# A graph network's own terms kept in on-chip memory, and its input tests moved one layer later

## The chip, the cores and the metric

The kernel runs on one core of a Trainium2 chip. The metric is the device time of one execution in microseconds; the median of nine runs before the change is 1521.09 us (1512.48 to 1530.87). TensorE (PE) multiplies matrices; VectorE (DVE), ScalarE (ACT) and GpSimd (POOL) do elementwise work; SyncE (SP) only issues transfers, and ACT and POOL issue some too, each on a queue of its own.

## The reference

Three graph layers run over 6250 nodes with 128 features and 200000 edges sorted by their target `dst`. Layer 0 is a message-passing layer with edge features, layers 1 and 2 are mean-aggregating (SAGE) layers inside a residual block:

```python
h = relu(layernorm(x))
x = x + relu(concat([h, segsum(h[src], dst), segsum(edge_attr, dst)]) @ W.T + b)
h = relu(layernorm(x))
h = relu(segsum(h[src], dst) / max(deg, 1) @ W1_l + b1 + h @ W1_r)      # layer 1
x = x + relu(segsum(h[src], dst) / max(deg, 1) @ W2_l + b2 + h @ W2_r)  # layer 2
```

Everything is float32. `dst` is drawn as 6250 times the square of a uniform number, so low nodes have many edges and high nodes few.

## The kernel before

**Blocks.** The nodes are cut into 49 blocks of 128. In a first phase (the build, up to about 600 us) the kernel counts on the chip how many edges lead from each node to each node, writes these counts to DRAM (`counts_d`), three counts packed in one 32-bit word, and sums the edges' features per target node into `aggE`, a tile of 128 partitions (features) by 49 x 128 nodes and some more columns. `aggE` lies in on-chip memory for the whole kernel.

**The three layers.** A layer's aggregation for a target block is a sum over the 49 source blocks of a matmul of counts with features. Forty blocks (`dense_order`) are done so in `neighbours` (L899): 49 matmuls (L944) of 256 columns, since each feature is split into a high and a low part (`terms`). The counts of a block come in one load of 1088 KB (`fetch`, L836, on SyncE's queue, four blocks ahead) and are cast from bytes to floats (`wide`, L876) by DVE and ACT in six pieces. The nine highest blocks have few edges; their rows are gathered by GpSimd (`gather`, L1025, 447 gathers in all) and summed by short matmuls (`sum_rows`, L1067) that are put among the dense ones at steps written out by hand (`at_step`, L1105). A gather waits for one of four buffers to be free.

**A block's chain.** `after` (L961) is a generator whose parts are issued at fixed steps of the next block. DVE adds the two halves of the sum (`y`, L969), multiplies by one over the degree and adds the *own part* `r` (L984; in layer 0 a plain add, L972). In layer 1 ACT applies Relu (`h`, L993), TensorE transposes `h` (L460), ACT copies it (`hT`, L462), and `times_weights` (L465) multiplies it by the two weight matrices of the next layer side by side (L467). The left half becomes that layer's features (`feats`, written to `rows_d` for the gathers), the right half plus the bias is the own part of that layer for the same block. In layer 2 nothing follows but Relu, the old `x` added, and the transfer to `out` on ACT's queue (L1004). So layer 2 has no transposes and no products behind its sums.

**The own part before.** Layer n makes the own part of layer n+1 in a buffer of three (`r`, L469), writes it to `r_d` in DRAM on SyncE's queue (L474), and `fetch_own` (L848) reads it back (`own`, L853) two blocks before layer n+1 adds it, also on SyncE's queue. There are 49 of these writes and 49 of these reads for each of the three layers, 64 KB each.

**aggE's uses.** In layer 0 one matmul per block multiplies the block's columns of `aggE` by the edge weights (L941, L1081). After layer 0 its first 4704 columns serve as scratch memory for the tests.

**The tests.** The build assumes things about the sorted edge list (how far targets spread within a stretch of edges, that the list is sorted, and more). `windows_right` (L1131) tests these: it loads the list of targets twice (784 KB each) into `aggE`, loads short rows into a small tile, and takes differences and maxima on DVE. It is a generator of 23 steps; one step is issued per dense block of layer 1, from the third on, behind that block's sum. Its transfers and three memsets are on GpSimd's queue, and `later` (L1010) puts each behind the newest gather. `all_right` (L1228) joins all tests to one bit, which goes to DRAM and back; it is issued early in layer 2, in three steps. At the 33rd dense block of layer 2 the engines load the bit (`trip`), and if it is set a slow general version computes everything again. With the inputs timed here it is not set.

**The order.** Every engine works through its instructions in the order in which they are written. A transfer that waits holds up all that stands behind it in its queue. Extra dependencies without a wait (`IN_ORDER`, `issue_after`) keep an instruction behind another of its engine.

Of the kernel before, what the change touches and what calls it, by code (L numbers as in the profile page):

```python
# [9 lines left out]
F32 = mybir.dt.float32  # L10
# [3 lines left out]
I32 = mybir.dt.int32  # L14
# [31 lines left out]
TESTS = 0  # L46
# [41 lines left out]
def kernel(ctx: ExitStack, tc: tile.TileContext, x, srcl, dstl, edge, w0t, b0, w1l, b1, w1r, w2l, b2, w2r, out):  # L88
# [11 lines left out]
    nc = tc.nc  # L100
# [6 lines left out]
    GU = G * U  # L107
    NR = len(REGIONS)
# [44 lines left out]
    r_d = [dram.tile([NP, D], F32, name=f"r{i}_d") for i in range(3)]  # L153
# [17 lines left out]
    unit_d = dram.tile([GU + 2], F32, name="unit_d")  # L171
    at_d = dram.tile([GU], F32, name="at_d")
# [9 lines left out]
    work = fast.enter_context(tc.tile_pool(name="work", bufs=2))  # L182
# [44 lines left out]
    at = once.tile([1, G, U], F32, name="at")  # L227
# [31 lines left out]
    for key, t in [*pick.items(), *pick_l.items()]:  # L259
        n = key if isinstance(key, int) else key[0]  # L260
        e = 16 * n
# [8 lines left out]
        empty = -(-unused // (P * n))  # L270
# [35 lines left out]
    apart = lambda t: t.rearrange("p (u g) -> p u g", u=U)  # L306
# [125 lines left out]
    def moments(xt):  # L432
        st = small.tile([P, 6], F32, name="st")
        nc.vector.bn_stats(st, xt)
        mv = small.tile([P, 2], F32, name="mv")
        nc.vector.bn_aggr(mv, st)
        return mv
# [27 lines left out]
    def times_weights(layer, b, hT, pz):  # L465
        at = slice(b * P, (b + 1) * P)
        mm = nc.tensor.matmul(pz, hT, w_sb[layer], start=True, stop=True)  # L467
        nc.scalar.copy(feats[:, slot_of[b], :], pz[:, :D])
        r = work.tile([P, D], F32, name="r", bufs=3)  # L469
        nc.vector.tensor_tensor(r, pz[:, D:], b_sb[layer], op=ALU.add)  # L470

        def write():
            nc.scalar.dma_start(rows_d[layer][at, :], feats[:, slot_of[b], :])
            nc.sync.dma_start(r_d[layer][at, :], r)  # L474

        return mm, write

# [221 lines left out]
    before = None  # L699
# [5 lines left out]
    for si, (g0, ng, n, w, k, sw, win) in enumerate(stretches):  # L705
# [6 lines left out]
        for g in range(g0, g0 + ng):  # L712
# [37 lines left out]
            for j in range(0, len(live), 2):  # L750
# [28 lines left out]
                for i, t0 in enumerate(units):  # L779
# [8 lines left out]
                    add = nc.gpsimd.tensor_tensor(to, to, fore[:, i, :], op=ALU.add)  # L788
# [25 lines left out]
        before = ring  # L814
# [19 lines left out]
    loaded, wide, own, sums, chains, waiting = {}, {}, {}, {}, {}, []  # L834
# [13 lines left out]
    def fetch_own(i):  # L848
        if isinstance(i, int) and i >= len(blocks):
            return  # L850
        layer, b = block_of(i)
        r = work.tile([P, D], F32, name="own", bufs=4)
        nc.sync.dma_start(r, r_d[layer][b * P : (b + 1) * P, :])  # L853
        own[i] = r

    def block_of(i):
        return blocks[i] if isinstance(i, int) else i
# [103 lines left out]
    def after(i):  # L961

        layer, b = block_of(i)
        at = i % NC if isinstance(i, int) else -1
        ps, r = sums.pop(i), own.pop(i)
        if layer == 0:
            nc.vector.tensor_copy(deg[:, b : b + 1], ps[:, NK * D : NK * D + 1])
        y = work.tile([P, D], F32, name="y", bufs=3)
        nc.vector.tensor_reduce(y, ps[:, : NK * D].rearrange("p (k f) -> p f k", k=NK), AX.X, ALU.add)  # L969
        if layer == 0:  # L970
            xt = xts.pop(i)
            nc.vector.tensor_tensor(y, y, r, op=ALU.add)  # L972
            nc.vector.scalar_tensor_tensor(xt, y, 0.0, xt, op0=ALU.max, op1=ALU.add)
            nc.sync.dma_start(x1_d[b * P : (b + 1) * P, :], xt)
            mv = moments(xt)
            yield
            pair = deviations(mv)
            yield
            next_layer(1, b, normed_to_rows(xt, pair), at < 0)
            if at == NC - 1:  # L980
                nc.vector.tensor_scalar(rdeg, deg, 1.0, None, op0=ALU.max)
                nc.vector.reciprocal(rdeg, rdeg)
            yield
        add = nc.vector.scalar_tensor_tensor(y, y, rdeg[:, b : b + 1], r, op0=ALU.mult, op1=ALU.add)  # L984
        if layer == 1:
            if at == TESTS:
                tests.append(windows_right())
            with tc.issue_after(add.ins):
                if at > TESTS + 1:
                    next(tests[0], None)  # L990
            yield
            h = work.tile([P, D], F32, name="h")
            nc.scalar.activation(h, y, AF.Relu)  # L993
            next_layer(2, b, h, at < 0)
            yield
            yield
        if at == 0:
            tests.append(all_right())
        elif at > 2:
            next(tests[1], None)  # L1000
        xt = xts.pop(i)
        nc.vector.scalar_tensor_tensor(xt, y, 0.0, xt, op0=ALU.max, op1=ALU.add)
        n = P if b + 1 < NB else last
        nc.scalar.dma_start(out[b * P : b * P + n, :], xt[:n, :])  # L1004
        yield
# [2 lines left out]
        (tail_waiting if listed else waiting).append((layer, b, h))  # L1008

    def later(it):  # L1010
        tc.add_manual_dep(it.ins, latest["POOL"].ins.name, IN_ORDER, reason="the first layer goes before the tests")
        return it


    latest, events, alone, tail_waiting, gathered, ready, tail_sums, tail_chain = {}, {}, {}, [], {}, {}, {}, []
# [93 lines left out]
    for layer in range(3):  # L1109
# [5 lines left out]
        for m, (_, _, marks) in enumerate(batches):  # L1115
            s = begin + (end - begin) * m // (len(batches) - 1)
# [14 lines left out]
    def windows_right():  # L1131

        dst, far = aggE[:, :GU], aggE[:, GU : 2 * GU]
        later(nc.gpsimd.dma_start(dst.bitcast(I32), dstl))
        yield
        nexts = aggE[:, 2 * GU : 3 * GU].bitcast(I32)
        later(nc.gpsimd.memset(nexts[P - 32 :, GU - U :], PAD))
        yield
        later(nc.gpsimd.dma_start(nexts[: P - 1, :], dstl[1:, :]))
        yield  # L1140
        later(nc.gpsimd.dma_start(nexts[P - 1 :, : GU - U], dstl[0:1, U:]))
        yield
        if unused:
            first_of_last = bass.AP(
                tensor=dstl.tensor, offset=dstl.offset + pad_p * GU + (G - 1) * U, ap=[[0, 1], [1, 1]]
            )
            later(nc.gpsimd.dma_start(nexts[P - 1 :, GU - 2 * U : GU - 2 * U + 1], first_of_last))
            yield


# [1 line left out]
        RU = RUN * U  # L1152
        assert NR * RU == GU
        rows = late.tile([NR, 5, RU], F32, name="rows")
        for i in range(3):
            later(nc.gpsimd.dma_start(rows[:, i], unit_d[i : i + GU].rearrange("(r e) -> r e", e=RU)))
            yield
        later(nc.gpsimd.dma_start(rows[:, 3], at_d.rearrange("(r e) -> r e", e=RU)))
        yield
        apart = 4  # L1160
        first_rows = (NR - 1) * RU
        later(nc.gpsimd.dma_start(
            rows[: NR - 1, 4], unit_d[1 + apart : 1 + apart + first_rows].rearrange("(r e) -> r e", e=RU)
        ))
        yield
        later(nc.gpsimd.dma_start(
            rows[NR - 1 :, 4, : RU - U - apart], unit_d[1 + apart + first_rows : 1 + GU - U].rearrange("(r e) -> r e", r=1)
        ))
        nothing = late.tile([1, U], F32, name="nothing")
        later(nc.gpsimd.memset(nothing, 0.0))  # L1170
        yield
        beyond = late.tile([1, U + apart], F32, name="beyond")
        later(nc.gpsimd.memset(beyond, float(2 * NP)))
        later(nc.gpsimd.dma_start(rows[NR - 1 :, 4, RU - U - apart :], beyond))
        yield
        nc.vector.tensor_copy(dst, dst.bitcast(I32))
        if unused:
# [41 lines left out]
        if unused:  # L1219

            empty = unused // P
            nc.gpsimd.dma_start(rows[NR - 1 :, 0, RU - U + 1 : RU - U + 1 + empty], nothing[:, :empty])
        yield
        yield
        for i, k in enumerate((0, 1, 3, 4)):
# [2 lines left out]
    def all_right():  # L1228

        highest = small.tile([P, 2], F32, name="highest")  # L1230
        nc.vector.tensor_reduce(highest[:, 0:1], worse, AX.X, ALU.max)
        nc.vector.tensor_reduce(highest[:, 1:2], deg, AX.X, ALU.add)
        yield
        for k, op in ((0, ALU.max), (1, ALU.add)):
            pf = psum.tile([P, 512], F32, name="pf", tag="pz")
            nc.tensor.transpose(pf[:1, :P], highest[:, k : k + 1], ident)
            nc.vector.tensor_reduce(bad[:, 4 + k : 5 + k], pf[:1, :P], AX.X, op)
        nc.vector.tensor_scalar(bad[:, 5:6], bad[:, 5:6], float(E), None, op0=ALU.not_equal)
        nc.vector.tensor_scalar(bad, bad, 0.5, None, op0=ALU.is_gt)
        again = small.tile([1, 1], F32, name="again")  # L1240
        nc.vector.tensor_reduce(again, bad, AX.X, ALU.max)
        again_i = small.tile([1, 1], I32, name="again_i")
        nc.vector.tensor_copy(again_i, again)
        yield
        again_d = dram.tile([1, 1], I32, name="again_d")
        nc.sync.dma_start(again_d, again_i)
        nc.sync.dma_start(trip_i, again_d)
# [18 lines left out]
    tests = []  # L1266
# [266 lines left out]
```

## Time and profile before

| | |
|---|---|
| median of nine runs | 1521.09 us |
| the profiled execution | 1519.39 us, span 1517.8 us |
| build | up to about 600 us |
| adds of the own part in layer 0 (L972), first to last | 605.1 to 906.3 us |
| first add of layer 1 (L984) | 920.1 us |
| layer 2, first to last out transfer | 1230.4 to 1513.0 us |
| tests in layer 1 | 937.7 to 1111 us |
| transfers on SyncE's queue: counts, own parts written, own parts read | 119 of 1088 KB, 147 of 64 KB, 147 of 64 KB |

The span runs from the first to the last recorded instruction. A view over a stretch of time gives, per engine, the busy time and in brackets the number of instructions; for TensorE that number divided by the length is the rate at which it really moves, because the length of one matmul in the records overlaps with the next. In lists of waits a line reads: who waited, at which line of the kernel, for whom, the total in us, how often, the longest. "issue" means that the profile shows nothing that the engine waited for.

### The profile page before, as it was taken

How to read it: one execution, taken by the hardware profiler on the slowest of the kernel's cores; microseconds unless marked ns; L12 is line 12 of the kernel's file. 1: busy time of each engine (PE TensorE's matmuls, PEld its weight loads, DVE VectorE, ACT ScalarE, POOL GpSimd, SP SyncE). 2: the span in 40 equal slices, each digit the busy share in tenths (PEclk: the TensorE clock that was granted, in tenths of full speed). 3: DMA queues.
4: the chain of work that ended last, by engine and by line, in shares of the span. 5: the costliest groups of instructions: out<-in, count | busy, mean ns of one | idle time of the engine just before them, and what ended most of it. 6: DMA issues, size and time to landing. Idle time of an engine off the chain costs nothing.

```text
span 1517.8 us, 37444 instructions
## 1 busy us (share of the span) xinstructions
PE 1426.7 (94%) x12457; PEld 1385.2 (91%) x12457; DVE 1151.1 (76%) x3006; ACT 931.6 (61%) x2253; POOL 685.5 (45%) x921
## 2 busy tenths in 40 slices
PE   7999999899999998999999997999899999998997
PEld 6899999798999997999899996999899989998897
DVE  8888899788998998677677774668666767675664
ACT  5434445467777777676676775666666766564563
POOL 4445667200000001666565605676666246576570
PEclk9999999999999999999999999999999999999999
DMA  2889898788999998777777765766666666676672
GB/s 79 283 267 300 279 322 319 270 299 309 311 315 343 332 354 306 264 239 230 233 227 224 234 207 195 241 223 201 205 224 215 199 202 219 215 248 198 213 250 63
DMA packets 173764, 374.02 MB, mean 246 GB/s; under 512 B 29451, under 2 KB 118985, under 8 KB 154234
## 3 DMA queue, kind: packets, MB, share of 16 engines
q1 hardware_dynamic: 121454, 268.72, 52.7%
q0 software_dynamic: 22336, 88.52, 17.2%
q10 hardware_dynamic: 29772, 14.31, 3.3%
q8 instruction: 100, 1.64, 0.4%
q14 instruction: 102, 0.84, 0.2%
HBM read 289.32 MB, written 82.13 MB: 245 GB/s over the span
## 4 chain that ended last, share of the span: by engine, by line
PE 66%; DMA 17%; issue 8%; DVE 3%; ACT 3%; another core or an unknown queue 1%; ACTq 0%; DVEq 0%; POOLq 0%; SPq 0%; POOL 0%
PE ps L944 43%; DMA counts_d<-ring 16%; PE pe L642 10%; PE ps_t L1077 4%; PE pz L467 3%; PE pu L755 2%; ACT wide L876 1%; PE pt L366 1%; PE pu L467 1%; PE pz L460 1%; DVE wide L876 1%; DMA src_i<-in_src 0%; DMA edge_t<-in_edge 0%; PE ps L941 0%
## 5 line engine op out<-in xcount | busy, mean ns | idle before, releaser
L944 PE MATMUL ps<-terms,wide 128*128 128x256 f32 (+1 forms) x5760 | 814.7, 293 | 19.8 <-issue 16.1
L944 PEld LDWEIGHTS ps<-terms,wide 128*128 128x128 f32 x5760 | 755.7, 200 | 30.0 <-issue 21.9
L1031 POOL DMA_INDIRECT rows_t<-rows_d,row_i x447 | 497.9, 1114 | 375.5 <-issue 112.6
L642 PE MATMUL pe<-hot,edge_t 128*128 128x128 f32 x3136 | 473.6, 288 | 3.1 <-DMA edge_t<-in_edge 2.0
L642 PEld LDWEIGHTS pe<-hot,edge_t 128*128 128x128 f32 x3136 | 396.3, 193 | 6.4 <-issue 2.2
L876 ACT CAST wide<-c 128x1024 fp32r<-128x1024 uint8 x239 | 284.7, 1205 | 131.5 <-PE ps L944 92.7
L781 ACT CAST ring<-pu 128x170 f32 (+5 forms) x736 | 205.7, 282 | 91.2 <-PE pu L766 44.9
L876 DVE CAST wide<-c 128x1024 fp32r<-128x1024 uint8 x241 | 174.2, 725 | 113.3 <-PE ps L944 89.8
L755 PE MATMUL pu<-sq,sp 128*128 128x102 bf16 (+7 forms) x1416 | 171.1, 219 | 15.5 <-DVE r L470 5.2
L876 ACT CAST wide<-c_early 128x1024 fp32r<-128x1024 uint8 x118 | 140.6, 1210 | 72.3 <-PE ps L944 54.1
L808 POOL DMA_DIRECT2D counts_d<-ring x50 | 27.3, 545 | 297.0 <-ACT ring L781 210.8
L788 POOL TENSOR_TENSOR ring<-ring,fore 128x17 int32 x280 | 118.4, 423 | 84.3 <-ACT fore L776 40.2
L520 DVE TENSOR_TENSOR sq<-iota,q_e 128x816 bf16<-128x816 f16 (+7 forms) x177 | 123.6, 699 | 8.5 <-PE pu L766 8.0
L876 DVE CAST wide<-c_early 128x1024 fp32r<-128x1024 uint8 x122 | 88.0, 722 | 55.4 <-PE ps L944 41.4
L755 PEld LDWEIGHTS <-sp 128*128 128x128 bf16 x1416 | 119.5, 99 | 10.4 <-DVE sq L531 3.5
L520 DVE TENSOR_TENSOR sp<-iota,p_e 128x1024 bf16<-128x1024 f16 x177 | 121.9, 688 | 4.5 <-PE pu L755 2.1
L1055 DVE TENSOR_TENSOR tw<-rows_t,tw 128x384 fp32r<-128x384 f32 x153 | 83.1, 543 | 33.6 <-ACT tw L1048 31.0
L766 PE MATMUL pu<-sc,sp 128*128 128x17 bf16 x745 | 96.2, 173 | 0.0
L633 DVE TENSOR_TENSOR hot<-iota,rel 128x64 f32<-128x64 f16 (+13 forms) x196 | 94.7, 485 | 0.0
L1077 PE MATMUL ps_t<-tw,hot_t 128*128 128x256 f32 (+1 forms) x483 | 85.5, 286 | 2.8 <-issue 2.8
L1049 DVE TENSOR_TENSOR hot_t<-iota_p,slot_e 128x384 fp32r<-128x384 f16 (+1 forms) x153 | 87.3, 571 | 0.0
L790 ACT CAST ring<-pu 128x68 f32 (+5 forms) x280 | 63.3, 248 | 38.1 <-ACT fore L776 15.3
(198 smaller groups left out, 1406.6 us busy)
## 6 DMA issues: line engine op xcount, KB each, us to landing
edge_t<-in_edge SPq DMA_DIRECT2D x196, 512.0 KB
c<-counts_d SPq DMA_DIRECT2D x80, 1088.0 KB
c_early<-counts_d SPq DMA_DIRECT2D x39, 1088.0 KB
rows_d<-feats ACTq DMA_DIRECT2D x147, 64.0 KB
r_d<-r SPq DMA_DIRECT2D x147, 64.0 KB
own<-r_d SPq DMA_DIRECT2D x147, 64.0 KB
counts_d<-ring POOLq DMA_DIRECT2D x5, 1462.0 KB
rows_t<-rows_d,row_i POOLq DMA_INDIRECT x447
```

Of the source, the lines that this page charges most:

```text
L520: made = nc.vector.tensor_tensor(to.rearrange("p t (c two) -> p t c two", two=2), iota[:, :m].rearrange("p (c two) -> p c two", two=2).uns ...
L633: nc.vector.tensor_tensor(hot[:, : U * win].rearrange("p (u w) -> p u w", w=win), iota[:, :win].unsqueeze(1).to_broadcast([P, U, win]), re ...
L642: mm = nc.tensor.matmul(ps[:, :P], e[:, u, :], hot[:, u * win : u * win + P], start=u == 0, stop=u == U - 1)
L755: mm = nc.tensor.matmul(pu[:, i * HALF : i * HALF + nq], sp[:, t, :], sq[:, t, :nq], start=t == t0, stop=t == t0 + n - 1 and n > 1,)
L766: mm = nc.tensor.matmul(pu[:, i * HALF : i * HALF + NJ], sp_b[:, t, :], sc[:, slot + 1 - len(last_tiles) + j0, :NJ], start=False, stop=j0 ...
L781: put = nc.scalar.copy(ring[:, bass.ds(to_put[(g - g0) * U + t0], nq)], pu[:, i * HALF : i * HALF + nq])
L788: add = nc.gpsimd.tensor_tensor(to, to, fore[:, i, :], op=ALU.add)
L876: copied = copy(t[:, : p1 - p0], two)
L944: dense = nc.tensor.matmul(ps[:, :m], counts, terms_of(s, s + 1)[:, 0, :m], start=s == 0, stop=s == NB - 1)
L1031: it = nc.gpsimd.indirect_dma_start(out=rows[:, u, :], out_offset=None, in_=rows_d[layer][:, :], in_offset=bass.IndirectOffsetOnAxis(ap=ro ...
L1049: made = nc.vector.tensor_tensor(hot[:, :k, :], iota_p.unsqueeze(1).to_broadcast([P, k, P]), slot_e[:, e : e + k].unsqueeze(2).to_broadcas ...
L1077: mm = nc.tensor.matmul(ps[:, :width], hot[:, k, :], tw[:, u, :width], start=begins, stop=ends)
```

## The change

The own part of layer 1 is written into the block's columns of `aggE` instead of a buffer, and read from there; its 49 writes to DRAM and 49 reads are not issued. Layers 0 and 2 keep theirs. As `aggE` now holds own parts until layer 1 is over, the tests of the edge list move to layer 2: one step per dense block from the third on, behind its sum; when `windows_right` has ended, the steps of `all_right` follow, also one per block. All transfers of the tests go on SyncE's queue instead of GpSimd's, without the order behind the gathers; the three memsets stay on GpSimd behind the newest gather.

```diff
         nc.scalar.copy(feats[:, slot_of[b], :], pz[:, :D])
-        r = work.tile([P, D], F32, name="r", bufs=3)
+        r = aggE[:, at] if layer == 1 else work.tile([P, D], F32, name="r", bufs=3)
         nc.vector.tensor_tensor(r, pz[:, D:], b_sb[layer], op=ALU.add)

         def write():
             nc.scalar.dma_start(rows_d[layer][at, :], feats[:, slot_of[b], :])
-            nc.sync.dma_start(r_d[layer][at, :], r)
+            if layer != 1:
+                nc.sync.dma_start(r_d[layer][at, :], r)
...
         layer, b = block_of(i)
+        if layer == 1:
+            own[i] = aggE[:, b * P : (b + 1) * P]
+            return
         r = work.tile([P, D], F32, name="own", bufs=4)
         nc.sync.dma_start(r, r_d[layer][b * P : (b + 1) * P, :])
...
         add = nc.vector.scalar_tensor_tensor(y, y, rdeg[:, b : b + 1], r, op0=ALU.mult, op1=ALU.add)
         if layer == 1:
-            if at == TESTS:
-                tests.append(windows_right())
-            with tc.issue_after(add.ins):
-                if at > TESTS + 1:
-                    next(tests[0], None)
             yield
             h = work.tile([P, D], F32, name="h")
             nc.scalar.activation(h, y, AF.Relu)
             next_layer(2, b, h, at < 0)
             yield
             yield
-        if at == 0:
-            tests.append(all_right())
-        elif at > 2:
-            next(tests[1], None)
+        if at == TESTS:
+            tests.extend((windows_right(), all_right()))
+        with tc.issue_after(add.ins):
+            if at > TESTS + 1:
+                if next(tests[0], True):
+                    next(tests[1], None)
         xt = xts.pop(i)
...
-        later(nc.gpsimd.dma_start(dst.bitcast(I32), dstl))
+        (nc.sync.dma_start(dst.bitcast(I32), dstl))
         yield
         nexts = aggE[:, 2 * GU : 3 * GU].bitcast(I32)
         later(nc.gpsimd.memset(nexts[P - 32 :, GU - U :], PAD))
         yield
-        later(nc.gpsimd.dma_start(nexts[: P - 1, :], dstl[1:, :]))
-        yield
-        later(nc.gpsimd.dma_start(nexts[P - 1 :, : GU - U], dstl[0:1, U:]))
+        (nc.sync.dma_start(nexts[: P - 1, :], dstl[1:, :]))
+        yield
+        (nc.sync.dma_start(nexts[P - 1 :, : GU - U], dstl[0:1, U:]))
         yield
...
         later(nc.gpsimd.memset(beyond, float(2 * NP)))
-        later(nc.gpsimd.dma_start(rows[NR - 1 :, 4, RU - U - apart :], beyond))
+        (nc.sync.dma_start(rows[NR - 1 :, 4, RU - U - apart :], beyond))
         yield
```

The other seven transfers of `windows_right` change their queue in the same way; its DVE operations are unchanged.

More of the change, by code (lines that the diff above doesn't have):

```diff
@@ L1010, in later @@
     def later(it):
-        tc.add_manual_dep(it.ins, latest["POOL"].ins.name, IN_ORDER, reason="the first layer goes before the tests")
+        tc.add_manual_dep(it.ins, latest["POOL"].ins.name, IN_ORDER, reason="the third layer's gathers go before the tests")
         return it
@@ L1146, in windows_right @@
             )
-            later(nc.gpsimd.dma_start(nexts[P - 1 :, GU - 2 * U : GU - 2 * U + 1], first_of_last))
+            (nc.sync.dma_start(nexts[P - 1 :, GU - 2 * U : GU - 2 * U + 1], first_of_last))
             yield
@@ L1155, in windows_right @@
         for i in range(3):
-            later(nc.gpsimd.dma_start(rows[:, i], unit_d[i : i + GU].rearrange("(r e) -> r e", e=RU)))
+            (nc.sync.dma_start(rows[:, i], unit_d[i : i + GU].rearrange("(r e) -> r e", e=RU)))
             yield
-        later(nc.gpsimd.dma_start(rows[:, 3], at_d.rearrange("(r e) -> r e", e=RU)))
+        (nc.sync.dma_start(rows[:, 3], at_d.rearrange("(r e) -> r e", e=RU)))
         yield
@@ L1161, in windows_right @@
         first_rows = (NR - 1) * RU
-        later(nc.gpsimd.dma_start(
+        (nc.sync.dma_start(
             rows[: NR - 1, 4], unit_d[1 + apart : 1 + apart + first_rows].rearrange("(r e) -> r e", e=RU)
@@ L1165, in windows_right @@
         yield
-        later(nc.gpsimd.dma_start(
+        (nc.sync.dma_start(
             rows[NR - 1 :, 4, : RU - U - apart], unit_d[1 + apart + first_rows : 1 + GU - U].rearrange("(r e) -> r e", r=1)
@@ L1221, in windows_right @@
             empty = unused // P
-            nc.gpsimd.dma_start(rows[NR - 1 :, 0, RU - U + 1 : RU - U + 1 + empty], nothing[:, :empty])
+            nc.sync.dma_start(rows[NR - 1 :, 0, RU - U + 1 : RU - U + 1 + empty], nothing[:, :empty])
         yield
```

## The prediction

> **What bounds the kernel now.** I read the page first: the span, the busy shares and the chain that ended last.
>
> ```profile
> span 1517.8 us, 37444 instructions
> PE 1426.7 (94%) x12457; PEld 1385.2 (91%) x12457; DVE 1151.1 (76%) x3006; ACT 931.6 (61%) x2253; POOL 685.5 (45%) x921
> ...
> PE 66%; DMA 17%; issue 8%; DVE 3%; ACT 3%; another core or an unknown queue 1%; ACTq 0%; DVEq 0%; POOLq 0%; SPq 0%; POOL 0%
> ```
>
> TensorE sets the pace; SyncE's and GpSimd's queues have 0% of the chain, and its DMA share belongs mainly to the counts that are written during the build (the chain's line for counts_d<-ring, 16%), which the change doesn't touch. So what the edit takes from queues pays only where TensorE waits in the same stage. The second view is therefore the busy time of each engine in stretches of layers 1 and 2, chosen by what the removed and moved steps do in them: 938 to 1110 us holds all the tests of edge lists (the first of their transfers is issued at 937.7, the last reduction runs at 1110.9).
>
> ```profile
> 938.00:950.00 12.00, 4.85 (x20) 3.83 (x19) 4.34 (x9) 3.29 (x6) 6.25 (x8) 0.68 0.42 122
> 950.00:1110.00 160.00, 151.59 (x1182) 148.77 (x1182) 112.97 (x270) 101.65 (x167) 107.72 (x102) 0.98 0.68 219
> 1110.00:1185.00 75.00, 72.19 (x572) 70.75 (x571) 50.03 (x111) 49.96 (x82) 46.13 (x43) 1.00 0.66 218
> 1185.00:1220.00 35.00, 35.00 (x280) 34.51 (x279) 26.18 (x53) 26.29 (x44) 0.93 (x1) 1.00 0.61 202
> ...
> 1220.00:1242.00 22.00, 22.00 (x182) 21.95 (x182) 15.91 (x32) 15.80 (x18) 8.11 (x8) 1.00 0.61 205
> 1242.00:1254.00 12.00, 8.39 (x36) 6.47 (x36) 2.51 (x6) 3.18 (x4) 7.27 (x8) 0.67 0.47 151
> 1254.00:1414.00 160.00, 152.07 (x1192) 150.01 (x1191) 106.06 (x240) 90.07 (x97) 106.77 (x93) 0.96 0.68 225
> ```
>
> The columns after the length are PE, weight loads, DVE, ACT and POOL, each with its count, then the clock, the DMA share and GB/s. Read the counts of PE as a rate. Layer 1 with tests and gathers runs 1182 / 160 = 7.39 matmuls per us, with gathers but no tests 572 / 75 = 7.63, with neither 280 / 35 = 8.00. Both layers open with a stall while the first gathers are issued without a pause: 20 matmuls in 12 us in layer 1, 36 in layer 2. Layer 2 reaches 8.27 per us before that and 7.45 in the 160 us behind it. The third view says what TensorE waits for: in 950 to 1110 us first, then in 1254 to 1414 us.
>
> ```profile
> PE pz L460 <- ACT h L993: 4.6, 2, 2.4
> PE pz L467 <- ACT hT L462: 3.6, 3, 2.1
> ...
> PE ps L944 <- issue: 6.3, 13, 0.9
> PE ps_t L1077 <- issue: 1.5, 2, 0.8
> ```
>
> In layer 1 it waits for a block's own chain (DVE's sum, ACT's Relu and copy, a transpose). Layer 2 has no such chain behind it, and its waits have no releaser at all. That is the asymmetry the forecast turns on.
>
> **The change, part by part.** All times are against the profiled execution: 1517.8 us of span in 1519.4 us, which is 1.7 us under the median of 1521.1.
>
> *49 writes of the own part in layer 0 and 49 reads in layer 1 go.*
>
> ```profile
> L474 SPq DMA_DIRECT2D r_d<-r x147: 235/326/1859, 49.5 to 1226.9; - x147
> L853 SPq DMA_DIRECT2D own<-r_d x147: 319/320/567, 64.7 to 1494.0; - x147
> ```
>
> SyncE loses 98 x 0.32 = 31 us of issuing and the waits for r and y in front of them, and 98 x 64 KB = 6.4 MB of 374 MB leave the transfers, about 26 us at the mean 246 GB/s. All of it lies beside other work: SPq is 0% of the chain, and TensorE's waits name no transfer of the own part. What is behind them on the queue is the load of counts, which takes its place when DVE frees a buffer, so it would only wait there instead. I take 0; the far end is a gain of 2 us, because the chain has one wait of 1.8 us on own<-r_d (at 870 us). The sum of r is the same DVE instruction (0.29 us) into another address; its buffer is the block that the matmul of layer 0 with the edges' weights read about two blocks earlier, so no new wait is late.
>
> *The tests leave layer 1.* On GpSimd that is 12 transfers, 0.57 to 1.16 us each, 7.7 us, and 11 us with the 0.3 us ahead of each; three memsets of 0.1 us move with them. On DVE I add the rows: the cast 0.98, three small ones 0.54, two subtractions 3.57, four maxima of rows 3.7, memsets and small maxima about 1, then 0.51, 1.58 and 1.77, eight operations on 14 rows 2.0 and four maxima 1.0: 16.6 us.
>
> ```profile
> L1189 DVE TENSOR_TENSOR aggE<-aggE,first x2: 1785/1786/1786, 1037.0 to 1052.6; 128x1568 f32<-128x1568 f32 x2
> ```
>
> What they cost TensorE comes from the rates: 1182 matmuls at 7.63 would take 155.0 us, so 5.0 us of 160. The two TensorE waits shown, 8.2 us in this stretch against 1.9 in the 75 us after it, say the same. The opening stall of layer 1 is 12 - 20 / 7.63 = 9.4 us long, that of layer 2, which has no test in it, 12 - 36 / 8.27 = 7.6 us; I give the difference, 1.7 us, to the 784 KB transfer issued at 937.7 among the gathers. Gain taken: 6.7 us. Ends: 0, if both were chance, and 14.4 us if the whole opening stall were that transfer's.
>
> *They arrive in layer 2.* 16.6 us of DVE, three memsets on GpSimd behind its newest gathers, and 12 transfers (1.6 MB) on SyncE at 0.32 us, 4 us of issue, one step per dense block, from the third block. Layer 2 lasts 282 us by its outputs (1230.4 to 1513.0), 7.07 us per dense block, so the 23 steps end near 1408 and the verdict is in memory by about 1425, some 30 us before the 33rd block, where the engines read it. Queued behind a test on SyncE are the own part, the old x and the counts. The two large loads landed 4.3 and 6.6 us after their issue, by the semaphores in the trace; the small one that follows a memset can hold SyncE for about 3 us, what GpSimd was behind DVE in layer 1 (memset at 1022.5, its block's sum at 1020). Cover: a load of counts in layer 2 is issued some 12 us before its first cast (the one issued at 1256.4 is cast from about 1268) and takes 4.6 us (the chain's piece at 688.5), so 7 us are free, and TensorE asks for that cast a block later still. DVE in 1254 to 1414 us is at 106 / 160 = 66%, under the 71% of layer 1's tests; its steps delay ACT's out transfer, and so ACT's casts, by up to 2.9 us in some blocks, under the same cover. Ends: 0, and 6.7 us, the price in layer 1. I take 2, nearer to the free end, because no wait of TensorE in layer 2 names ACT or DVE.
>
> At this place a rule speaks against the change. The Trainium skill, "DMA: Bandwidth & Descriptors", section "Issuing engines are not separate DMA queues", says that transfers issued from different engines end on the same 16 DMA engines and that changing the issuer saves issuing time only. If the cost of the tests is in their transfers, it then moves to layer 2 whole and the sum would be 0 instead of minus 4.7. No view here separates the two; the rates above price the tests as a whole.
>
> *The two steps of the verdict* (two transposes, six small DVE operations, two transfers) move from the start of layer 2 behind the tests: the same instructions in the same layer, 0, covered by the 30 us above.
>
> Sum: 0 - 6.7 + 2 + 0 = -4.7 us: 1514.7 us against the profiled run, **1516.4 us** against the median.
>
> **The rivals.** *The cost only changes its layer (hidden anyway).* Layer 2 charges what layer 1 saves: 0, 1521. For it: layer 2 at 7.45 matmuls per us is already no better than layer 1 without tests. Against it: the waits shown are of different kinds.
>
> *Layer 2's unexplained stalls multiply (slower).* Its rate of 8.27 would need 144 us for the 1192 matmuls that took 160, so 16 us are lost in stalls with no releaser, while GpSimd issues gathers and counts are loaded; the clock column falls to 0.96. If the 1.6 MB and DVE's long operations add half as much again, that is +8; with nothing saved in layer 1, 1529. It decides when the added stalls pass 6.7 us. Against it: layer 0 runs 2284 matmuls in the 300 us from 605 (7.61 per us) at a DMA share of 0.72, higher than layer 2's, with the clock at 1.00.
>
> *The opening stall was the 784 KB load.* All 14.4 us come back and layer 2 charges 2: 1509. Against it: layer 2's opening is nearly as bad without a test.
>
> *The change doesn't do what it says*: if the scheduler took the shared memory for one object, writing r would wait for the last matmul that read any of it; that matmul runs blocks ahead, so it costs nothing here.
>
> **How the numbers follow.** Of 1521, half a per cent is 7.6 us, about what a measurement of this kernel can tell from no change. Forecast, a gain of 2 to 10 us: 0.40. Cost changes its layer, -2 to +5: 0.18. Stalls multiply, +5 to +14: 0.25. Opening stall goes, -10 to -16: 0.17. Of the forecast's share a third (0.13) lies beyond a gain of 7.6, of the stalls' share 0.03 within a loss of 7.6. So faster 0.17 + 0.13 = 0.30, slower 0.22, same 0.48. The forecast's own range is 1511 to 1519. For 8 in 10 the range takes in the fast case to 1506 and the slow one to 1531.
>
> **What would show it.** Right: layer 1 between its opening and the end of its gathers at 7.6 matmuls per us, waits for hT and h near 2 us per 75; own<-r_d and r_d<-r at x98; aggE<-in_dst on SPq in layer 2; layer 2's 160 us behind its opening at 7.35 or more. Wrong: layer 1 still at 7.4, or the issue waits of L944 in layer 2 well above 14 us, or a wait of TensorE for a cast of counts there.

## The result, and the profile after

The changed kernel takes 1542.47 us (median of 20 executions, 1532.97 to 1553.33), the kernel before 1522.98 (62 executions). The ratio is 1.0148 with an interval of 1.0127 to 1.0169 (the two medians alone give 1.0128): slower, by 19 to 26 us on 1522.98. Ratios, here and below, leave out executions more than 1.5% above the fastest of the same kernel. The prediction was 1516.4 us with a range of 1506 to 1531, so its sign and its range are both wrong.

The profiled execution took 1536.36 us, with a span of 1534.8. Its page, the same lines as before:

```profile
span 1534.8 us, 37165 instructions
PE 1430.7 (93%) x12457; PEld 1388.1 (90%) x12457; DVE 1151.2 (75%) x3006; ACT 932.0 (61%) x2253; POOL 692.2 (45%) x909
...
PE 77%; DMA 7%; issue 4%; ACT 4%; DVE 3%; POOL 1%; another core or an unknown queue 1%; ACTq 0%; SPq 0%; DVEq 0%; POOLq 0%
PE ps L948 41%; PE pe L643 21%; PE pu L756 4%; PE ps_t L1078 3%; PE pz L467 3%; DMA counts_d<-ring 3%; DMA c<-counts_d 2%; PE pu L467 2%; ACT ring L782 1%; ACT wide L880 1%; PE pt L366 1%; DMA x_c<-in_x 1%; PE pz L460 1%; DVE wide L880 1%
```

TensorE is busy 4 us longer, the span is 17.0 us longer. New among the chain's large lines is a transfer: `c<-counts_d`, the load of a block of counts, with 2% of the span. The share of the build's `counts_d<-ring` in this chain (16% before, 3% now) says nothing on the change: a chain is one path out of several. (The changed file has a few more lines: L944 of before is L948 here, L876 is L880, L655 is L656, L853 is L857, L1139 is L1140.)

The busy time in stretches shows where the time went. The columns are the stretch, its length, then PE, weight loads, DVE, ACT and POOL with their counts, the clock, the DMA share and GB/s. First layer 1, in the same stretches as before:

```profile
950.00:1110.00 160.00, 152.22 (x1186) 148.57 (x1186) 102.55 (x221) 102.38 (x168) 98.66 (x90) 0.99 0.60 199
1110.00:1185.00 75.00, 74.63 (x592) 73.36 (x592) 50.51 (x110) 52.44 (x88) 45.74 (x42) 1.00 0.67 227
```

With no operation of the tests on DVE or GpSimd in it, the first stretch has 1186 matmuls in 160 us, 7.41 per us, where it had 1182. The expected 7.63 did not come. Then the opening of layer 2:

```profile
1216.00:1241.00 25.00, 24.94 (x206) 24.81 (x205) 16.77 (x34) 16.39 (x19) 11.22 (x11) 1.00 0.69 232
1241.00:1253.00 12.00, 6.36 (x27) 4.79 (x26) 2.71 (x7) 2.56 (x4) 7.69 (x9) 0.70 0.25 68
1253.00:1272.00 19.00, 19.00 (x148) 19.00 (x148) 9.90 (x21) 8.40 (x9) 9.28 (x9) 0.92 0.36 116
1272.00:1294.00 22.00, 0.86 (x6) 0.66 (x5) 2.75 (x6) 3.56 (x4) 0.16 (x1) 0.60 0.36 123
1294.00:1414.00 120.00, 118.27 (x945) 116.07 (x945) 97.50 (x242) 72.59 (x79) 93.19 (x73) 0.99 0.72 241
```

The stall of 1241 to 1253 was there before. The one of 1272 to 1294 is new: TensorE does 6 matmuls in 22 us, and behind it runs at 945 / 120 = 7.88 per us, though DVE does the tests there. The waits from 1254 to 1300 us (engine and line, what it waited for, us in total, times, longest) name the cause:

```profile
ACT wide L880 <- DMA c<-counts_d: 24.6, 1, 24.6
DVE wide L880 <- DMA c<-counts_d: 24.0, 1, 24.0
...
PE ps_t L1078 <- DVE tw L1056: 21.1, 1, 21.1
```

One wait, once: ACT and DVE wait for a load of counts. Each works in order. The gathered rows' high parts (`tw`, L1049, on ACT) and low parts (`tw`, L1056, on DVE) stand behind these casts, and TensorE's short matmul waits for the low parts. SyncE's queue around it (start, length of the issuing instruction, what):

```profile
1250.89 0.25 SPq L1140 DMA_DIRECT2D aggE<-in_dst  x1
1253.56 0.34 SPq L656 DMA_DIRECT2D c<-counts_d  x1
1257.32 12.46 SPq L857 DMA_DIRECT2D own<-r_d  x1
1269.87 1.99 SPq L1265 DMA_DIRECT2D xt<-x_d  x1
1271.96 1.83 SPq L656 DMA_DIRECT2D c<-counts_d  x1
...
1290.41 0.33 SPq L656 DMA_DIRECT2D c_early<-counts_d  x1
```

The load of counts is issued at 1253.56 and is there at 1290.3, 36.8 us later; the one that the prediction read took 4.6. Ahead of it in the queue is one transfer of the tests: L1140, the target list moved by one row, `dstl[1:, :]`, 127 rows of 6272 bytes. The packet records of the trace show its 127 packets one behind the other from 1251.8 to 1287.2 us, most of them 0.235 to 0.26 us apart and some up to 0.5. Of the 128 packets of the load of counts behind it, 120 started between 1254.5 and 1258.2 us; the last eight, one sixteenth, started between 1287.2 and 1289.5, directly behind the 127. So most of that load went past the slow transfer, and the load was held up by one share in 16. The 12.46 us of the next issue and the 1.8 to 3.1 us of those behind it fall into the same time. On GpSimd's queue, before, the same transfer was issued at 954.9 us and its packets ran from 956.3 to 964.2, up to 17 at once: 9.3 us from issue to last packet.

So the theory to test, A, is this: a direct transfer of 127 rows from SyncE's queue goes through one of the 16 DMA engines, and the share of that engine in a load behind it on the queue comes after it. The rivals: B, SyncE's queue was held by the tests' waits and the work beside it, whatever the shape; C, the cost is a growth of layer 2's waits without a releaser, the slower rival of the prediction.

### The profile page after: what moved, and what is told of

Its sections match the earlier page's. It is cut to its first block, busy times and chain, and to the rows that moved or that the text cites. A ratio compares the mean times of both kernels' runs of the same rounds, so it can differ in the third digit from the quotient of the medians.

```text
span 1534.8 us, 37165 instructions
## 1 busy us (share of the span) xinstructions
PE 1430.7 (93%) x12457; PEld 1388.1 (90%) x12457; DVE 1151.2 (75%) x3006; ACT 932.0 (61%) x2253; POOL 692.2 (45%) x909
## 4 chain that ended last, share of the span: by engine, by line
PE 77%; DMA 7%; issue 4%; ACT 4%; DVE 3%; POOL 1%; another core or an unknown queue 1%; ACTq 0%; SPq 0%; DVEq 0%; POOLq 0%
PE ps L948 41%; PE pe L643 21%; PE pu L756 4%; PE ps_t L1078 3%; PE pz L467 3%; DMA counts_d<-ring 3%; DMA c<-counts_d 2%; PE pu L467 2%; ACT ring L782 1%; ACT wide L880 1%; PE pt L366 1%; DMA x_c<-in_x 1%; PE pz L460 1%; DVE wide L880 1%
## 5 line engine op out<-in xcount | busy, mean ns | idle before, releaser
L948 PE MATMUL ps<-terms,wide 128*128 128x256 f32 (+1 forms) x5760 | 817.5, 293 | 17.3 <-issue 13.4
L948 PEld LDWEIGHTS ps<-terms,wide 128*128 128x128 f32 x5760 | 757.9, 200 | 27.1 <-issue 19.2
L1032 POOL DMA_INDIRECT rows_t<-rows_d,row_i x447 | 513.0, 1148 | 390.7 <-DVE tw L1056 119.7
L880 ACT CAST wide<-c 128x1024 fp32r<-128x1024 uint8 x239 | 285.3, 1206 | 151.8 <-PE ps L948 86.4
L880 DVE CAST wide<-c 128x1024 fp32r<-128x1024 uint8 x241 | 174.5, 728 | 129.5 <-PE ps L948 84.2
L880 ACT CAST wide<-c_early 128x1024 fp32r<-128x1024 uint8 x118 | 140.5, 1206 | 61.9 <-PE ps L948 47.7
L880 DVE CAST wide<-c_early 128x1024 fp32r<-128x1024 uint8 x122 | 87.8, 721 | 45.5 <-PE ps L948 42.4
L1056 DVE TENSOR_TENSOR tw<-rows_t,tw 128x384 fp32r<-128x384 f32 x153 | 83.4, 545 | 35.9 <-ACT tw L1049 30.6
L1078 PEld LDWEIGHTS ps_t<-tw,hot_t 128*128 128x128 f32 x483 | 70.2, 192 | 25.1 <-DVE tw L1056 22.0
```

The lines of the kernel that those rows point to most:

```text
L880: copied = copy(t[:, : p1 - p0], two)
L948: dense = nc.tensor.matmul(ps[:, :m], counts, terms_of(s, s + 1)[:, 0, :m], start=s == 0, stop=s == NB - 1)
L1032: it = nc.gpsimd.indirect_dma_start(out=rows[:, u, :], out_offset=None, in_=rows_d[layer][:, :], in_offset=bass.IndirectOffsetOnAxis(ap=ro ...
L1078: mm = nc.tensor.matmul(ps[:, :width], hot[:, k, :], tw[:, u, :width], start=begins, stop=ends)
```

## The experiments

Each experiment was timed beside the kernel before on its own chip; the kernel before took 1517 to 1539 us on the chips used, so only ratios are compared.

**The transfer in two pieces.** One line of the changed kernel, all on SyncE's queue as before:

```diff
-        (nc.sync.dma_start(nexts[: P - 1, :], dstl[1:, :]))
+        (nc.sync.dma_start(nexts[:112, :], dstl[1:113, :]))
+        (nc.sync.dma_start(nexts[112 : P - 1, :], dstl[113:, :]))
```

> The changed kernel with one edit: the load of the target list shifted by one row (127 rows of 6272 bytes, on SyncE's queue) is cut into one of 112 and one of 15 rows on the same queue. Theory A (a transfer of 127 rows from SyncE's queue moves row after row through one of the 16 DMA engines, and the load of counts behind it shares that engine): the 21 us wait of TensorE for the low parts of gathered rows is gone, counts land in 4.5 us again, ratio to the kernel before 0.995 to 1.002. Rival B (SyncE's queue is held by the waits of the tests, whatever their shape): the 21 us stay, ratio 1.012 to 1.017. Rival C (layer 2's stalls without a releaser grow with the tests): ratio 1.004 to 1.012, with issue waits of L948 well above 14 us.

Measured: 1533.24 us, ratio 0.9976 (0.9937 to 1.0015). The packets of the two pieces run from 1267.4 to 1275.0 us, and no wait of a cast there names a load of counts. SyncE's queue, then TensorE's waits in layer 2 (1240 to 1540 us):

```profile
1266.42 0.33 SPq L1140 DMA_DIRECT2D aggE<-in_dst  x1
1266.86 0.37 SPq L656 DMA_DIRECT2D c<-counts_d  x1
1267.28 0.43 SPq L1141 DMA_DIRECT2D aggE<-in_dst  x1
1270.71 0.34 SPq L857 DMA_DIRECT2D own<-r_d  x1
```

```profile
PE ps L948 <- issue: 16.2, 34, 1.1
PE ps_t L1078 <- issue: 3.5, 8, 0.9
PE ps_t L1078 <- DVE tw L1056: 1.2, 2, 0.6
```

The same bytes on the same queue at the same step: the 21 us wait is gone, and with it the loss, as far as the interval tells. By B or C this edit would have changed nothing.

**Only that transfer back on GpSimd's queue.** The other eleven stay on SyncE's.

```diff
-        (nc.sync.dma_start(nexts[: P - 1, :], dstl[1:, :]))
+        later(nc.gpsimd.dma_start(nexts[: P - 1, :], dstl[1:, :]))
```

> The changed kernel with that one transfer of 127 rows back on GpSimd's queue behind the newest gather, the eleven others still on SyncE's. A: it lands in about 6.6 us as in the kernel before, no 21 us wait, ratio 0.995 to 1.002. B: 11 of 12 transfers still hold SyncE, so about half of the loss or more stays, 1.006 to 1.015. C: as the changed kernel without its one long wait at most, 1.004 to 1.012.

Measured: 1540.29 us beside 1537.44, ratio 1.0004 (0.9966 to 1.0041). The 127 packets run from 1270.1 to 1274.1 us, and the longest wait of TensorE in layer 2 for DVE's low parts is 3.4 us. A again: one transfer of twelve carries the loss.

**Only that transfer on SyncE's queue, in the kernel before.** The own part, the other transfers and the tests stay where they were, in layer 1.

```diff
-        later(nc.gpsimd.dma_start(nexts[: P - 1, :], dstl[1:, :]))
+        nc.sync.dma_start(nexts[: P - 1, :], dstl[1:, :])
```

> The kernel before with one edit: the transfer of 127 rows in layer 1 goes on SyncE's queue; the own part still goes through DRAM, all other tests stay on GpSimd in layer 1. A: the same stall appears in layer 1 near 955 us: counts behind it land after 30 us or more, TensorE stops some 20 us, ratio 1.010 to 1.017. B and C, which need the other eleven transfers or layer 2: ratio 0.997 to 1.004.

Measured: 1574.73 us (6 executions), ratio 1.0222 (1.0163 to 1.0280). SyncE's queue, then the waits from 984 to 1016 us:

```profile
968.38 0.25 SPq L1139 DMA_DIRECT2D aggE<-in_dst  x1
968.74 13.88 SPq L655 DMA_DIRECT2D c_early<-counts_d  x1
982.71 0.38 SPq L474 DMA_DIRECT2D r_d<-r  x1
983.84 5.98 SPq L853 DMA_DIRECT2D own<-r_d  x1
```

```profile
DVE wide L876 <- DMA c_early<-counts_d: 28.5, 1, 28.5
...
PE pz L460 <- ACT h L993: 24.9, 1, 24.9
```

The load of counts directly behind it takes 39.2 us by the chain, and TensorE stands for 24.9. Of that load, too, 120 of 128 packets had started by 987.2 us, and the last eight started between 1004.8 and 1007.1, behind the 127. The loss is larger than in layer 2 and than the 1.010 to 1.017 expected. The load stands closer behind, 0.36 us against 2.67, and TensorE stands once more for 6.8 us (L467, no releaser shown); whether these make up the difference was not tested. The stall needs neither layer 2 nor the other moves; it belongs to the one line.

**The transfer by itself.** Behind the end of the kernel before, where nothing else moves, six loads of the target list follow one another, each waiting for the one ahead:

```diff
+    for q, n in ((nc.sync, 128), (nc.sync, 127), (nc.sync, 126), (nc.sync, 120), (nc.gpsimd, 127), (nc.scalar, 127)):
+        it = q.dma_start(aggE[:n, :GU].bitcast(I32), dstl[:n, :])
```

> The kernel before, and behind its end six further loads of the target list into the memory of the edge sums, one after another, each waiting for the one ahead: 128, 127, 126 and 120 rows of 6,272 bytes on SyncE's queue, 127 on GpSimd's, 127 on ScalarE's. A (a load of 127 rows from SyncE's queue goes through one of 16 DMA engines, whatever else runs): 128 rows 3 to 5 us, 127 rows 28 to 36 us, 126 and 120 rows 3 to 7 us, 127 rows on GpSimd's queue 4 to 7 us, on ScalarE's 28 to 36 us. B (the queue was merely held by work beside it): all six 3 to 7 us, as nothing else moves there.

The issues on the three queues, in order of time; the distance from one to the next is what a load took:

```profile
1517.20 0.33 SPq L1305 DMA_DIRECT2D aggE<-in_dst  x1
...
1521.43 0.25 SPq L1305 DMA_DIRECT2D aggE<-in_dst  x1
...
1553.29 0.33 SPq L1305 DMA_DIRECT2D aggE<-in_dst  x1
...
1557.82 0.33 SPq L1305 DMA_DIRECT2D aggE<-in_dst  x1
...
1563.94 0.58 POOL L1305 DMA_DIRECT2D aggE<-in_dst  x1 [68.36 <-SPq L1312]
...
1570.02 0.26 ACTq L1305 DMA_DIRECT2D aggE<-in_dst  x1
```

This was one execution with each load once. From SyncE, 128 rows take 4.2 us, 127 rows 31.9, 126 rows 4.5 and 120 rows 6.1; from GpSimd 127 rows take 6.1; from ScalarE they land at 1601.96, 31.9 us after the issue. One row less than 128 costs a factor of 7.5. The stretches inside the 127-row load of SyncE, the 126-row load, GpSimd's and ScalarE's (the last two columns are the DMA share and GB/s):

```profile
1522.50:1552.50 30.00, 0.00 (x0) 0.00 (x0) 0.00 (x0) 0.00 (x0) 0.00 (x0) 0.50 0.06 26
1554.30:1557.30 3.00, 0.00 (x0) 0.00 (x0) 0.00 (x0) 0.00 (x0) 0.00 (x0) 0.50 0.68 249
1565.20:1569.30 4.10, 0.00 (x0) 0.00 (x0) 0.00 (x0) 0.00 (x0) 0.00 (x0) 0.50 0.84 196
1571.00:1601.00 30.00, 0.00 (x0) 0.00 (x0) 0.00 (x0) 0.00 (x0) 0.00 (x0) 0.50 0.06 26
```

A share of 0.06 is one engine of 16. The landing events in the trace count the engines as well: 16 of them for SyncE's 128 rows and for GpSimd's 127; one just after the issue and then 14 for 126 rows, 15 for 120 rows, and a single one for 127 rows from SyncE (1553.28 us) and from ScalarE (1601.96). This settles A against B: with nothing else moving, the queue and the row count together set the time.

**All tests on GpSimd's queue, own part on chip, in layer 2.** The change without its new queue, run on two chips:

```diff
-        (nc.sync.dma_start(dst.bitcast(I32), dstl))
+        later(nc.gpsimd.dma_start(dst.bitcast(I32), dstl))
...
-        (nc.sync.dma_start(nexts[: P - 1, :], dstl[1:, :]))
+        later(nc.gpsimd.dma_start(nexts[: P - 1, :], dstl[1:, :]))
...
```

> The changed kernel with all twelve transfers of the tests on GpSimd's queue in layer 2, each behind the newest gather as the kernel before had them in layer 1; the own part of layer 1 stays on chip. A: no 21 us wait, ratio 0.995 to 1.002; the prediction's sum for the rest of the change says 0.997. C: 1.004 to 1.012, since tests and gathers still meet in layer 2. B: as A here, so e1 tells A from B.

> The own part on chip and the tests in layer 2 on GpSimd's queue, a second time: the version that might beat the kernel before. Under O1 0.994 to 0.998 again, under O0 0.998 to 1.002.

Measured: ratio 0.9963 (0.9925 to 1.0001), then 0.9926 (0.9890 to 0.9962). The mean of each kernel's executions over that of the kernel before beside it gives 0.9963 over both, with 0.0019 either way (1.96 standard errors of both sides): about 5.6 us faster than the kernel before, and the only complete version here that the runs put below it. C falls here too. TensorE's waits without a releaser in layer 2 (L948) are 21.0 us in the first profile and 13.5 in the second, 11.1 with the own part through DRAM, 14.1 in the kernel before and 15.0 in a kernel without any test: they scatter between executions by more than the tests add, and the kernel with 21.0 is not slower.

**The test move alone.** As the last, but r stored to DRAM and loaded again as in the kernel before.

> The own part through DRAM as in the kernel before; the twelve transfers of the tests in layer 2, on GpSimd's queue: the place of the tests is changed and neither their queue nor the own part. A (the loss of the change is the transfer of 127 rows on one DMA engine of SyncE's queue; the place of the tests is worth little): ratio 0.995 to 1.001, and like that of the own part on chip with the tests on GpSimd's queue (0.996). B2 (the gain against before in that kernel came from the own part on chip): ratio 1.000 to 1.004 here, 0.004 above that kernel. r_d and own move x196 in all here, x98 there.

Measured: 1514.51 us, ratio 0.9988 (0.9959 to 1.0018). Moving the tests one layer on, on their old queue, is worth nothing that can be told. (By the means, the version with the own part on chip is 0.26% below this one, with 0.28% either way.)

**Both kernels without the tests.** One line more in each:

```diff
     def windows_right():
+        return
```

> The changed kernel (own part on chip) without the window tests of the edge lists: their transfers and operations are left out, and so is the part of the computation that tells whether the lists' windows are in order. A: without the tests the 21 us wait is gone, ratio 0.993 to 0.998. B2 (the own part on chip is worth something by itself): 0.004 or more below the same with the own part through DRAM. If neither place nor own part is worth anything: ratio 0.995 to 1.000, the same in both.

> The kernel before (own part through DRAM) without the window tests of the edge lists; the same part of the computation is left out. It gives the worth of the tests on the old place by itself: ratio 0.993 to 0.999 (the prediction had them at 6.7 us, 0.9956). Against the same with the own part on chip: A expects a difference within 0.002, B2 0.004 or more.

Measured on one chip: 0.9941 (0.9911 to 0.9970) with the own part on chip, 1.0009 (0.9978 to 1.0040) through DRAM. The second says that the tests cost layer 1 almost nothing. The first was a surprise: without tests, little but the own part divides the two kernels, and their medians differ by 0.44% (1507.90 to 1514.63 us) where the prediction had 0. The profiles don't explain it. The first is 9.9 us ahead of its partner already at layer 0's last sum (894.9 against 904.8 us), 3 us of it at that layer's first add (600.1 against 603.2). TensorE has the same instructions up to there; SyncE has 49 writes fewer. But in the second pair below the two last sums lie at 909.6 and 909.5 us, so that lead is not the own part's in general. So both were run again, with a third kernel that carries the own part's traffic three times:

```diff
             nc.sync.dma_start(r_d[layer][at, :], r)
+            if layer == 1:
+                for more in more_d:
+                    nc.sync.dma_start(more[at, :], r)
...
         nc.sync.dma_start(r, r_d[layer][b * P : (b + 1) * P, :])
+        if layer == 1:
+            for k, more in enumerate(more_d):
+                c = (b + 24 * k) % NB * P
+                nc.sync.dma_start(aggE[:, c : c + P], more[b * P : (b + 1) * P, :])
```

> The kernel before without the window tests (that part of the computation is left out), and each of the own part's transfers of layer 1 three times: two more stores to further DRAM arrays, two more loads into the idle memory of the edge sums, 196 further DMAs of 64 KB on SyncE's queue. O0 (the own part's 98 DMAs cost nothing, as the prediction had them): within 0.3% of the same kernel without the further ones. O1 (their removal is worth the 0.44% that the two kernels without tests differed by): 0.5 to 1.3% above it.

> The changed kernel without the window tests (that part of the computation is left out), a second time, on one chip with its partner. O0: within 0.25% of the kernel before without the tests; the 0.44% of the first pair was chance (its profiled execution is 10 us shorter in layer 0, where both have the same instructions). O1: 0.3 to 0.7% below it again.

> The kernel before without the window tests (that part of the computation is left out), a second time: the partner of the two above. Against before: ratio 0.997 to 1.002, as the first time (1.0009); the prediction's 6.7 us for the tests in layer 1 would be 0.9956.

Measured: 0.9979 (0.9944 to 1.0013) with three times the traffic, 0.9945 (0.9908 to 0.9981) with the own part on chip, 0.9976 (0.9936 to 1.0016) with it through DRAM. By these ratios the further 196 transfers cost nothing (O0), yet the pair differs by 0.31% again (O1). The means of the same executions say otherwise: three times the traffic is 0.32% above its partner, with 0.32% either way, and the pair is 0.04% apart. So this set decides nothing between O0 and O1. A last run on another chip keeps the transfers and takes away the waits for them: r is stored and loaded again, but the sums read it on chip.

```diff
-            if layer != 1:
-                nc.sync.dma_start(r_d[layer][at, :], r)
+            nc.sync.dma_start(r_d[layer][at, :], r)
...
             own[i] = aggE[:, b * P : (b + 1) * P]
+            unread = work.tile([P, D], F32, name="own", bufs=4)
+            nc.sync.dma_start(unread, r_d[layer][b * P : (b + 1) * P, :])
             return
```

> The changed kernel without the window tests (that part of the computation is left out), with the own part's 98 transfers of layer 1 put back as idle traffic: r is stored from the memory of the edge sums and loaded into a buffer that nothing reads. T (the transfers and SyncE's issues cost the 0.3 to 0.4%): like the kernel before without the tests, within 0.2%. W (the wait of the dense sum for its load and of r for its buffer cost it): like the changed kernel without the tests, within 0.2%. N (the own part is worth nothing): all three within 0.2%.

> The changed kernel without the window tests (that part of the computation is left out), a third time: T and W 0.992 to 0.997 of before, N 0.997 to 1.001.

> The kernel before without the window tests (that part of the computation is left out), a third time: 0.997 to 1.001 of before under T, W and N.

Measured: 0.9964 (0.9933 to 0.9995), 0.9968 (0.9934 to 1.0001) and 0.9973 (0.9946 to 1.0000). All three are within 0.1%, which is N. By the means over the kernel before beside it, 34 and 33 executions over three chips, the own part on chip is 0.31% below the same through DRAM, with 0.20% either way (0.9956 and 0.9987): 5 us, with 3 either way. The gain is probably there, but small, and most of it comes from the first pair. The pairs are too far apart, and the last set too inconclusive, to say whether it comes from the transfers or from the waits. That stays open.

## Why the prediction was wrong, step by step

**The own part, taken at 0 with a far end of 2 us.** The counts came as said:

```profile
L475 SPq DMA_DIRECT2D r_d<-r x98: 319/326/1419, 50.0 to 1222.1; - x98
L857 SPq DMA_DIRECT2D own<-r_d x98: 319/326/12458, 64.8 to 1510.5; - x98
```

That the transfers lie beside other work at no cost is not shown: 196 more of them cost 0.03% by the ratios and 0.32% by the means, each within its noise. The size was probably off: 5 us of gain with 3 either way, where the far end was 2. No wait in the views accounts for it.

**"The tests leave layer 1", taken at 6.7 us of gain.** This fell. The kernel before without any test is 0.13% faster by the means of the three pairs, 0.15% either way, so the tests cost 0 to 4 us there. The 5.0 us were a difference of rates, 7.39 against 7.63 matmuls per us, between two stretches of one execution. In the changed kernel, without tests in layer 1, the first stretch ran at 7.41 and the second at 7.89; in the kernel before without any test at 7.39 (1182 in 160 us) and 7.80 (585 in 75). The stretches differ by themselves, and I had put the difference down to the tests. The 1.7 us for the opening stall is not borne out either: from 905 to 950 us the kernel before did 251 matmuls, the changed kernel, which issues the 784 KB load elsewhere (at 1151.7 us), 248, and the kernel before without any test 249.

**"They arrive in layer 2", taken at 2 us.** This is the step that decided. It set against the loads of counts a cover of 7 us, because "the two large loads landed 4.3 and 6.6 us after their issue". Those two times were from GpSimd's queue, and the change moves the transfers to SyncE's. The 784 KB load of 128 rows can be moved so (4.2 us there by the probe); the one of 127 rows cannot (31.9 us there, 6.1 from GpSimd). The 6.6 us was also a misreading: it is the first of that transfer's landing events (961.56 us); the last came at 964.82, 9.9 us after the issue, which is already more than the 7 us of cover. A second term of the step, SyncE held for about 3 us by the small transfer that follows a memset, was too small as well:

```profile
SPq L1175 <- POOL beyond L1174: 7.6, 1, 7.6
```

No wait of TensorE shows these 7.6 us; what hurt was the 127-row transfer, during which SyncE was also held 12.46 us in one issue. The cover itself was read rightly: the first cast that waited began to wait 36.8 - 24.6 = 12.2 us after the issue of its load, as the step had it. TensorE was to ask a block (7 us) later; it stood 36.8 - 21.1 = 15.7 us after, 3.5 us behind the cast, because the parts of the gathered rows stood behind the casts. With the load at 36.8 us there was no cover left. The order was also not as the step had it: of the tests' twelve transfers only the three behind a memset came in layer 2 (1250.9, 1350.2 and 1403.8 us); six were issued at 587 to 590 us, ahead of layer 0, and three at 1151.7 to 1215.2 us, in layer 1. Without the order behind the gathers they were not held to their place in the text; with it, on GpSimd's queue, all twelve came between 1258.2 and 1412.2 us in the first of the two runs.

The rule that I weighed at this place, that the issuing engine changes only the issuing time, is one that this transfer breaks: the same bytes took 31.9 us from SyncE and 6.1 from GpSimd. The same page of the Trainium skill, "DMA: Bandwidth & Descriptors", has the rule that tells it, in the section "Why a DMA increments its semaphore by 16 and not by 1": a transfer is given to the largest number of engines, up to 16, that divides the slowest dimension of both its patterns, so that 127 rows get one engine, except that GpSimd's direct copies were seen to use all 16 in some cases. This case agrees on each point that it shows: a share of 0.06 from SyncE and ScalarE, 0.84 from GpSimd, and from SyncE 16, 1, 14 and 15 landing events for 128, 127, 126 and 120 rows. I read that page for the queue and not for the shape.

**The verdict's steps, taken at 0.** TensorE's only wait that names them is 0.3 us (`pf`, L1237). This held.

**The rivals.** "Layer 2's unexplained stalls multiply" had the right sign and the wrong mechanism: TensorE's waits without a releaser in layer 2 (the dense sums' line) were 14.1 us before and are 12.5 now. TensorE's waits in layer 2 of the changed kernel:

```profile
PE ps_t L1078 <- DVE tw L1056: 21.6, 2, 21.1
PE ps L948 <- issue: 12.5, 21, 1.5
```

"The cost only changes its layer" is nearest to the truth for the tests on GpSimd's queue (0.9988), though with hardly a cost to move. "The opening stall was the 784 KB load" fell with the 248 and 249 matmuls. That the scheduler takes the shared memory for one object showed no sign.

**What was named as a sign of being wrong.** Two of the three signs came: layer 1 still at 7.4, and TensorE behind a cast of counts (by way of the low parts of gathered rows). The third, growing waits of L944, did not. Of the signs of being right only the x98 came, and one of the four transfers `aggE<-in_dst` in layer 2 on SyncE's queue: the waits for h and hT from 950 to 1110 us are 7.1 us (3.2 and 3.9), 8.2 before.

**The sum as measured.** 1.48% or 22.5 us of loss. The 127-row transfer on SyncE's queue costs 1.4 to 1.9% of the time by the three kernels that take its single engine away (1.0148 less 1.0004, 0.9976 and 0.9963), 22 to 28 us, of which 21.1 us are shown as one wait. All the rest of the change is then a gain of 0 to 0.4%.

## What to carry to other kernels

Before a transfer is moved to another queue, look at its rows as well as its bytes: from SyncE's and ScalarE's queues 127 rows took 31.9 us where 128 from SyncE took 4.2, and a load behind it on SyncE's queue waited for it. Cut into 112 and 15 rows, the same transfer cost nothing that can be told. A transfer has landed with the last of its landing events, not with the first. A landing time read in the trace belongs to the queue that it was read on. A difference of rates between two stretches of one execution is not the price of what lies in one of them; a run without that work gives the price.

## What the runs showed of the hardware

A 127-row load of 777.9 KB from SyncE or ScalarE moves at 26 GB/s, on one of 16 DMA engines, with nothing else moving. On SyncE's queue it holds up a load behind it by that engine's share alone: 120 of 128 packets of the load of counts went past it, eight came behind it, and the load took 36.8 us in one kernel and 39.2 in another instead of 4.6. SyncE's own issuing instructions, 0.32 us as a rule, took up to 12.46 and 13.88 us meanwhile; why is not shown. GpSimd's queue with the same 127 rows used most of the engines (0.84).
